# LSTM states stored batch-major, row loads spread over the first stage, and two norm steps moved, in a four-layer graph network

## The chip, the cores and the metric

The kernel runs on one core of one Trainium2 chip. The metric is the device time of one execution in microseconds (us). The kernel before takes 2278.68 us in the median of three runs (2278.61 to 2280.02).

The engines named below: TensorE (PE; PEld is its weight load), VectorE (DVE), ScalarE (ACT), GpSimd (POOL), and SyncE (SP), which here only issues DMAs. Each takes its instructions in the order in which the program holds them. SP and POOL have a DMA queue each.

## The reference, cut to what matters

The input `x` has 128 batches of 64 nodes with 256 features, float32 throughout; `adj` is 64 x 64. Four layers follow each other, and each adds its result to `x` and normalizes the rows.

```
x = layernorm(x + L0(x))   # three times: adj*adj applied to x @ W, relu between   (256 -> 512 -> 1024 -> 256)
x = layernorm(x + L1(x))   # U, the eigenvectors of the normalized Laplacian: U @ (relu(U.T @ x @ W1 + b1) @ W2 + b2)
x = layernorm(x + L2(x))   # below
x = layernorm(x + L3(x))   # attention between the 64 nodes, masked by adj
```

Layer 2, which holds the states that the change is about:

```
h = relu(adj @ (x @ Wg0 + bg0))
h = relu(adj @ (h @ Wg1 + bg1))
for p in 1, 2, 3, 4:                       # T = 64 nodes
    nw = T // p
    wins = h[:, :nw * p].reshape(B * nw, p, H)      # windows of p neighbouring nodes
    last = lstm_last(Wih[p], Whh[p], ..., wins)     # p steps, gates i, f, g, o; zero state first
    h[:, p - 1 : nw * p : p] = last                 # the last node of each window is replaced
```

So step t of a window of p nodes reads every p-th node of `h`, beginning with node t, and the last step's result is written to every p-th node.

## The kernel before, in words

**Rows and groups.** The 128 x 64 rows are 64 tiles of 128 rows (two batches each). Four tiles, eight batches, are a group; there are 16 groups. The rows of four groups stay in `X`, those of the other twelve are loaded to `XA` (lines 893 to 906).

**First stage: layer 0 and the eigenvectors.** `layer0` (line 1164) goes through the 16 groups in the order `order`, 4 to 15 and then 0 to 3. For each it computes the three products of layer 0, the two large ones by a scheme of seven block products in place of eight (`seven`, line 1101), which needs sums and differences of blocks. Those of the third product are made in the tile `sh`, of four slots, by DMA: SP copies one slot to another and a block of `h2` to a slot (lines 1182 and 1183), and POOL's queue issues DMAs that add to them (`adds`, line 1059). PE's product 5 of `by_third` (line 1097) is the first that reads `sh`. `mix_rows` (line 1138) adds the result to the rows, queues their normalization, and has SP store the rows of twelve groups to DRAM (`rest`, line 1153). In the gaps of PE and DVE runs `eigen` (line 275), a generator that computes the eigenvectors of the 64 x 64 matrix in small steps.

**Loads.** Before any of that the kernel issues all its loads on SP's queue (lines 910 to 959): the weights of layer 0, all 16 groups' rows in 128 KB pieces (`fetch`, line 904), then `eig_c` (constants of `eigen`), and the weights and biases of the later layers through `load` (line 888). The order of the instructions of PE, DVE, ACT and POOL in this stage is the order of the code (`tc.manual_schedule`, line 1227); SP's is chosen by the framework's scheduler.

**Second stage: layers 1 to 3.** The weights of the LSTMs are loaded, and then a planner (`Plan`, line 104) orders everything. Work is noted with a cost in us for each instruction (`Noted`, line 251; some have a `cost=` of their own), grouped in units of two groups of rows, and `Plan.run` (line 164) places up to four units' instructions by readiness and due time. Line 162, `emit`, therefore stands for all instructions of this stage in the profile. SP is planned too: loads and stores of rows, and `across` (line 1521), which sends a tile through DRAM to complete a transpose.

**The states.** `to_lstm` (line 1480) computes `h` transposed: features on the 128 partitions (two halves, `k`), and 512 columns for 64 nodes and 8 batches. These columns are stored node first: column 8n + b. The ReLU that writes them (`relu_out`, line 1500) turns them from batch-major, so it writes one element every 8. `singles`, `pairs` and `long` (lines 1774, 1781, 1791) run the LSTMs of windows of 1, 2, and 3 or 4 nodes; `long` takes the two groups of a unit at once. Each step is one call of `fast` (line 1679), which again uses seven products in place of eight on the two halves of features and two halves of columns: three of the seven read the state itself as the moving operand (the one that streams through PE, `moving[1..3]`), the others sums made by four subtractions on DVE. The hidden state `hs` between steps is a tile of its own and contiguous. The result goes to the state by `turn_out` (line 1770).

**Back to rows.** `from_lstm` (line 1534) turns the state to rows. For groups 0 to 13 DVE transposes 32 x 32 blocks, reading the state batch by batch (every 8th element), and `across` does the rest. For the last two groups, `ENDING`, the state is first copied batch-major, by two copies of DVE and two of ACT a group, and PE transposes the copy. `norm` (line 1434) normalizes two tiles: statistics on DVE, `(variance + eps) ** -0.5` on POOL in two steps (`rs`), and, for the last groups' `scalar` form, two more POOL steps for `nm`, minus the mean times `rs`, before ACT applies both.

Of the kernel before, what the change touches and what calls it, by code (L numbers as in the profile page):

```python
# [11 lines left out]
F32 = mybir.dt.float32  # L12
AF = mybir.ActivationFunctionType
ALU = mybir.AluOpType
# [762 lines left out]

RING = 4
QUADS = 1.17

# [60 lines left out]
def kernel(  # L841
# [74 lines left out]
    for h in range(2):  # L916
        cols = slice(h * 512, (h + 1) * 512)
        nc.sync.dma_start(aw2[:, :, cols], a_w2.rearrange("(k p) f -> p k f", p=P)[:, :, cols])
    for g in order[1:]:
        for u in range(2):  # L920
            fetch(nc.sync, g, u)
        if g == order[1]:
            aw3 = load(wa, "aw3", a_w3, "(k p) f -> p k f", [P, 8, D], p=P)
    nc.sync.dma_start(eig_c, consts)

# [24 lines left out]
    cb1 = keep.tile([P, 2], F32, name="cb1")  # L950
    nc.sync.dma_start(cb1, c_b1)
    wide = {}
    for name, src in (("b_b1", b_b1), ("b_b2", b_b2), ("c_b0", c_b0), ("d_b", d_b)):
        wide[name] = keep.tile([P, src.shape[0]], F32, name=f"wide_{name}")
        nc.sync.dma_start(wide[name], src.partition_broadcast(P))
    cbi = keep.tile([P, 4, 8], F32, name="cbi")
    cbh = keep.tile([P, 4, 8], F32, name="cbh")
    nc.sync.dma_start(cbi, c_bi)
    nc.sync.dma_start(cbh, c_bh)

# [203 lines left out]
    def layer0():  # L1164
# [12 lines left out]
        for g in range(n):  # L1177
            last = g == n - 1
            then = {} if last else {
                (1, 1): lambda: less(2, 0, 0),  # L1180
# [46 lines left out]
    with tc.manual_schedule(engines={mybir.EngineType.PE, mybir.EngineType.DVE, mybir.EngineType.Activation,  # L1227
                                     mybir.EngineType.Pool}):
        pt = bank()
        PE.transpose(pt[:N, :P], adst, ident)  # L1230
        for h in range(2):
            hs = slice(h * N, (h + 1) * N)
            V.tensor_copy(adT2[hs, hs], pt[:N, hs])
        V.tensor_mul(sqT2, adT2, adT2)
        layer0()
        while eig:
            now[0] = max(now[0], eig[0])
            between()
# [22 lines left out]
    few = ctx.enter_context(tc.tile_pool(name="few", bufs=1, reuse_waits="tile"))  # L1261
    psb = ctx.enter_context(tc.tile_pool(name="psb", bufs=1, space=bass.MemoryType.PSUM, reuse_waits="tile"))
    wih, whh = [], []
    for i in range(4):
# [169 lines left out]
    def norm(x, scalar, eps=EPS, twice=False):  # L1434
        st, mv, rs = plan.tile("st", [P, 2, 6]), plan.tile("mv", [P, 2, 2]), plan.tile("rs", [P, 2])
        for t in range(2):
            V.bn_stats(st[:, t, :], x[:, t, :])
            V.bn_aggr(mv[:, t, :], st[:, t, :])
        if twice:
            G.tensor_scalar(rs, mv[:, :, 1], eps, 0.25, op0=ALU.add, op1=ALU.mult)  # L1440
        else:
            G.tensor_scalar(rs, mv[:, :, 1], eps, None, op0=ALU.add)
        G.tensor_tensor(rs, rs, half[:, :2], ALU.pow, cost=0.74)
        if scalar:
            nm = plan.tile("nm", [P, 2])
            G.tensor_scalar(nm, mv[:, :, 0], -1.0, None, op0=ALU.mult)
            G.tensor_tensor(nm, nm, rs, ALU.mult)
        for t in range(2):
            if scalar:
                S.activation(x[:, t, :], x[:, t, :], AF.Identity, bias=nm[:, t:t + 1], scale=rs[:, t:t + 1], cost=0.5)  # L1450
            else:
                V.tensor_scalar(x[:, t, :], x[:, t, :], mv[:, t, 0:1], rs[:, t:t + 1], op0=ALU.subtract,
                                op1=ALU.mult)
# [26 lines left out]
    def to_lstm(xs, there):  # L1480
# [9 lines left out]
        a = mixed(g1, adT2)  # L1490
        hT = plan.tile("w", [P, 1024]).rearrange("p (k n b) -> p k n b", k=2, b=8)
        b = [[a[:, k, w * D:(w + 1) * D] for w in range(2)] for k in range(2)]
# [7 lines left out]
        def relu_out(c):  # L1500
            S.activation(hT[:, c, :, :].rearrange("p n b -> p b n"), hs[c].rearrange("p w (a n) -> p (w a) n", n=N),
                         AF.Relu, scale=2.0, cost=0.933)

# [30 lines left out]
    def from_lstm(xs, hT, g):  # L1534
        if g in ENDING:
            hb = as3(work(), 2)
            for bs in (slice(0, 4), slice(4, 8)):
                for k, copy, cost in ((0, V.tensor_copy, 0.33), (1, S.copy, 0.56)):
                    copy(as3(hb[:, k, :], 8)[:, bs, :], hT[:, k, :, bs].rearrange("p n b -> p b n"), cost=cost)
            for t in range(0, 4, 2):  # L1540
                p = ps4((P, 2, D))
                turns([(p[:, j, k * P:(k + 1) * P], hb[:, k, (t + j) * P:(t + j + 1) * P]) for j in range(2)
                       for k in range(2)])
                V.tensor_add(xs[:, t:t + 2, :], p, xs[:, t:t + 2, :])
                norm(xs[:, t:t + 2, :], True, 4 * EPS)
            return
        z = work()
        for k in range(2):
            V.transpose(z.rearrange("p (j t k f) -> p t j k f", j=4, t=4, k=2)[:, :, :, k],
                        hT[:, k].rearrange("p n b -> p b n"), cost=1.0)  # L1550
        y = across(z).rearrange("p (i m f) -> p m i f", i=4, m=8)
        for t in range(0, 4, 2):
            x2 = xs[:, t:t + 2, :].rearrange("p t (k i f) -> p (t k) i f", k=2, i=4)
            V.tensor_add(x2, y[:, 2 * t:2 * t + 4], x2)
            norm(xs[:, t:t + 2, :], False, 4 * EPS)
# [123 lines left out]
    def fast(p, n, x, hs=None, c=None, new=None, write=None):  # L1679
# [8 lines left out]
        def parts(v):  # L1688
            return v.rearrange("p (r b) -> p r b", b=8)

# [79 lines left out]
    def turn_out(dst, o, t):  # L1770
        o, t = (v.rearrange("p (r b) -> p r b", b=8) for v in (o, t))
        V.scalar_tensor_tensor(dst, o, 1.0, t, op0=ALU.add, op1=ALU.mult)

    def singles(hT):

        def write(h, o, t):
            turn_out(hT[:, h], o.rearrange("p w n -> p (w n)"), t.rearrange("p w n -> p (w n)"))

        fast(1, 256, [[hT[:, k, 32 * w:32 * w + 32, :] for w in range(2)] for k in range(2)], write=write)

    def pairs(hT):

        def write(h, o, t):
            turn_out(hT[:, h, 1:64:2, :], o.rearrange("p w n -> p (w n)"), t.rearrange("p w n -> p (w n)"))

        x = [[[hT[:, k, 32 * w + t:32 * w + 31 + t:2, :] for w in range(2)] for k in range(2)] for t in range(2)]
        c, hs = state("c"), state("hs")
        fast(2, 128, x[0], c=c, new=hs)
        fast(2, 128, x[1], hs=hs, c=c, write=write)

    def long(hTs, p):
# [3 lines left out]
        def seen(h, w, t):  # L1795
            return hTs[w][:, h, t:t + (nw - 1) * p + 1:p, :]

        def write(h, o, t):
            for w in range(2):
                turn_out(seen(h, w, p - 1), o[:, w], t[:, w])  # L1800

# [103 lines left out]
```

## Time and profile before

| what | value |
|---|---|
| median of three runs | 2278.68 us |
| profiled execution | 2278.08 us |
| its span, first to last instruction | 2276.3 us |
| mean granted TensorE clock | 0.991 |
| busy PE, PEld, DVE, ACT, POOL | 2215.7, 2035.9, 1758.0, 1241.8, 209.9 us |
| DMA | 163.10 MB, mean 72 GB/s |
| first stage | from 0 to some 822 us |
| second stage | from some 829 us to the end |

The span is what the profiled execution's engines did; 1.8 us of its time lie around it. PE's busy time counts each record of a matmul; a float32 matmul of this kernel is two records, each with a weight load of its own. Records overlap, so the spacing of their starts tells what one costs, and their duration is longer.

In the first two of the page's 40 slices (57 us each) 216 and 104 GB/s are moved, afterwards mostly 100 or less.

### The profile page before, as it was taken

To read this page: it belongs to the slowest core of one execution; us is meant where nothing else is said; L and a number is where in the kernel's file an instruction comes from. 1 tells how busy PE (TensorE), PEld (TensorE's weight loads), DVE (VectorE), ACT (ScalarE), POOL (GpSimd) and SP (SyncE) were. 2 spreads that over 40 slices of the span, in tenths; PEclk is the share of its full clock that TensorE was granted. 3 is DMA by queue.
4 is the path that set the end of the run, shared out by engine and by line. 5 is a ranking of instruction groups with operands and counts; after the bars stand their busy time and mean duration, and the time that the engine had idled before them with its cause. 6 is when DMAs were issued, how large, how long until landed. Compare 5 with 4: busy or idle time off the path is not lost.

```text
span 2276.3 us, 53986 instructions
## 1 busy us (share of the span) xinstructions
PE 2215.7 (97%) x21256; PEld 2035.9 (89%) x21256; DVE 1758.0 (77%) x5911; ACT 1241.8 (55%) x2999; POOL 209.9 (9%) x390
## 2 busy tenths in 40 slices
PE   8699999999999999999999999999999999999996
PEld 6688998888898878999999999999999999999995
DVE  6588878777888859765967977976976886668986
ACT  3255555545555445665655665655655656566554
POOL 0011111111111110000100000000010010000112
PEclk9899999999999999999999999999999999999998
DMA  7434333334433231000111211311221221002441
GB/s 216 104 93 100 87 76 85 78 81 101 96 85 75 66 135 48 20 1 20 66 44 37 85 57 42 94 57 41 87 66 41 78 75 38 13 11 71 130 122 44
DMA packets 95741, 163.10 MB, mean 72 GB/s; under 512 B 25472, under 2 KB 66432, under 8 KB 95488
## 3 DMA queue, kind: packets, MB, share of 16 engines
q1 hardware_dynamic: 84320, 120.05, 16.5%
q0 software_dynamic: 10800, 39.33, 9.1%
q8 instruction: 167, 2.74, 0.5%
q14 instruction: 86, 0.70, 0.1%
q10 hardware_dynamic: 368, 0.28, 0.0%
HBM read 57.64 MB, written 45.09 MB: 45 GB/s over the span
## 4 chain that ended last, share of the span: by engine, by line
PE 84%; DVE 8%; SPq 2%; DMA 2%; ACT 1%; issue 1%; POOL 1%; DVEq 0%; ACTq 0%; POOLq 0%
PE ps L162 55%; PE ch L977 15%; PE b L977 7%; PE ps L977 4%; PE ps L1070 2%; SPq L906 2%; DVE X L162 1%; DVE w L162 1%; DVE gates L162 1%; DVE D L52 1%; PE pa L312 1%; POOL rs L162 1%; DVE st L162 1%; PE ps L1143 1%; DMA aw<-in_a_w_dram 1%
## 5 line engine op out<-in xcount | busy, mean ns | idle before, releaser
L162 PE MATMUL ps<-w,wih 128*128 128x128 f32 (+2 forms) x2944 | 574.4, 299 | 4.7 <-DVE gates L162 2.0
L162 PEld LDWEIGHTS ps<-w,wih 128*128 128x128 f32 x2944 | 453.0, 191 | 32.4 <-DVE gates L162 6.8
L162 PE MATMUL ps<-w,sums 128*128 128x128 f32 (+2 forms) x3104 | 474.6, 294 | 0.2 <-DVE w L162 0.2
L162 PEld LDWEIGHTS ps<-w,sums 128*128 128x128 f32 x3104 | 421.9, 192 | 13.7 <-ACT gates L162 1.9
L162 ACT ACTIVATE gates<-gates,cbi 128x256 f32<-128x256 f32 (+4 forms) x736 | 318.0, 482 | 179.0 <-DVE gates L162 177.0
L162 DVE TENSOR_TENSOR gates<-gates,ps 128x512 f32<-128x512 f32 (+4 forms) x408 | 236.2, 586 | 159.0 <-PE ps L162 138.4
L162 ACT COPY gates<-ps 128x512 f32<-128x512 f32 (+4 forms) x408 | 205.2, 508 | 264.0 <-PE ps L162 258.8
L986 ACT ACTIVATE h<-h 128x512 f32<-128x512 f32 x141 | 89.0, 632 | 275.6 <-DVE h L52 275.0
L162 PE MATMUL ps<-hs,whh 128*128 128x128 f32 (+1 forms) x896 | 181.4, 284 | 0.2 <-DVE hs L162 0.2
L162 PE MATMUL ps<-w,whh 128*128 128x128 f32 (+1 forms) x896 | 181.2, 284 | 0.0
L162 POOL TENSOR_SCALAR rs<-mv 128x2 f32<-128x2 f32 x96 | 30.8, 329 | 1319.4 <-DVE mv L162 1317.7
L162 ACT ACTIVATE gates<-ps,cbi 128x128 f32<-128x128 f32 (+2 forms) x368 | 120.9, 385 | 40.9 <-PE ps L162 39.8
L162 PEld LDWEIGHTS ps<-hs,whh 128*128 128x128 f32 x896 | 139.7, 191 | 0.5 <-DVE hs L162 0.5
L162 PEld LDWEIGHTS ps<-w,whh 128*128 128x128 f32 x896 | 139.7, 191 | 0.0
L977 PE MATMUL b<-ss,aw 128*128 128x256 f32 x512 | 122.5, 379 | 0.0
L977 PE MATMUL ch<-m,tw 128*128 128x256 f32 x512 | 120.3, 380 | 0.0
L977 PEld LDWEIGHTS ch<-m,tw 128*128 128x128 f32 x512 | 96.4, 190 | 13.3 <-DVE h L52 0.4
L977 PEld LDWEIGHTS b<-ss,aw 128*128 128x128 f32 x512 | 96.5, 190 | 12.8
L1060 POOL DMA_DIRECT2D sh<-h x60 | 53.3, 959 | 503.9 <-ACT h L986 214.3
L162 PE MATMUL ps<-hs,sums 128*128 128x128 f32 (+1 forms) x448 | 90.6, 284 | 0.0
L162 ACT ACTIVATE gates<-c 128x256 f32<-128x256 f32 (+1 forms) x176 | 76.1, 435 | 24.5 <-DVE c L162 22.4
L162 DVE TENSOR_TENSOR w<-w,w 128x128 f32<-128x128 f32 (+2 forms) x264 | 79.6, 316 | 8.3 <-PE ps L162 6.6
(385 smaller groups left out, 4266.2 us busy)
## 6 DMA issues: line engine op xcount, KB each, us to landing
sh<-h POOLq DMA_DIRECT2D x60, 512.0 KB, 5.7
far<-w SPq DMA_DIRECT2D x42, 512.0 KB, 2.9
w<-far SPq DMA_DIRECT2D x168, 128.0 KB, 3.1
X<-rest SPq DMA_DIRECT2D x24, 512.0 KB, 3.7
out_dram<-X SPq DMA_DIRECT2D x64, 128.0 KB, 2.4
sh<-sh SPq DMA_DIRECT2D x15, 512.0 KB, 2.9
sh<-h SPq DMA_DIRECT2D x15, 512.0 KB, 2.9
sh<-sh POOLq DMA_DIRECT2D x15, 512.0 KB, 4.6
```

The source lines that it names most:

```text
L52: return getattr(self.engine, name)(out, *args, **kw)
L162: getattr(e, name)(*[real(x) for x in args], **{k: real(v) for k, v in kw.items()})
L312: PE.matmul(out, lhsT, rhs, start=True, stop=True)
L906: queue.dma_start(rows_of(g)[hs, 2 * u:2 * u + 2, :], given[2 * g + u, h])
L977: PE.matmul(out, lhsT, rhs, start=start, stop=stop, **kw)
L986: S.activation(dst, src, AF.Relu)
L1060: nc.gpsimd.dma_start(out, src, accum_op=ALU.add)
L1070: PE.matmul(p[h][m, k, t, :], src[hs, t, f], sqT2[hs, hs], start=True, stop=True)
L1143: PE.matmul(p[h][js, u, :], sqT2[hs, hs], s3[hs, 2 * u + j, :], start=True, stop=True)
```

## The change

The states are stored batch first, column 64b + n. The ReLU's write, the transposes of groups 0 to 13, and the transposes of the last groups then read or write contiguous columns, and the four copies a group before the latter are gone. In exchange a step's columns of a window of p nodes lie p elements apart: reads by PE and DVE and the writes of the last step.

In `norm`'s scalar form, `variance + eps` and `nm` (now one instruction) are on DVE; the power stays on POOL.

In the first stage only the first four groups' rows are loaded ahead (`AHEAD`). The others are issued at the head of the steps, four groups ahead, and so are the loads of constants, two a step. SP's order is now that of the code there too.

```diff
+AHEAD = 4
@@ loads
-    for g in order[1:]:
+    for g in order[1:AHEAD]:
         for u in range(2):
             fetch(nc.sync, g, u)
         if g == order[1]:
             aw3 = load(wa, "aw3", a_w3, "(k p) f -> p k f", [P, 8, D], p=P)
-    nc.sync.dma_start(eig_c, consts)
+    later = [(eig_c, consts)]
+
+    def load(pool, name, src, pattern, shape, **kw):
+        t = pool.tile(shape, F32, name=name)
+        later.append((t, src.rearrange(pattern, **kw)))
+        return t
...
-    nc.sync.dma_start(cb1, c_b1)
+    later.append((cb1, c_b1))
...
@@ layer0
         for g in range(n):
             last = g == n - 1
+            if g + AHEAD < n:
+                for u in range(2):
+                    fetch(nc.sync, order[g + AHEAD], u)
+            for to, of in later[2 * g:2 * g + 2]:
+                nc.sync.dma_start(to, of)
...
     with tc.manual_schedule(engines={mybir.EngineType.PE, mybir.EngineType.DVE, mybir.EngineType.Activation,
-                                     mybir.EngineType.Pool}):
+                                     mybir.EngineType.Pool, mybir.EngineType.SP}):
@@ norm
-        if twice:
+        if scalar:
+            V.tensor_scalar(rs, mv[:, :, 1], eps, None, op0=ALU.add)
+        elif twice:
             G.tensor_scalar(rs, mv[:, :, 1], eps, 0.25, op0=ALU.add, op1=ALU.mult)
         else:
             G.tensor_scalar(rs, mv[:, :, 1], eps, None, op0=ALU.add)
         G.tensor_tensor(rs, rs, half[:, :2], ALU.pow, cost=0.74)
         if scalar:
             nm = plan.tile("nm", [P, 2])
-            G.tensor_scalar(nm, mv[:, :, 0], -1.0, None, op0=ALU.mult)
-            G.tensor_tensor(nm, nm, rs, ALU.mult)
+            V.scalar_tensor_tensor(nm, mv[:, :, 0], -1.0, rs, op0=ALU.mult, op1=ALU.mult)
@@ to_lstm
-        hT = plan.tile("w", [P, 1024]).rearrange("p (k n b) -> p k n b", k=2, b=8)
+        hT = plan.tile("w", [P, 1024]).rearrange("p (k b n) -> p k b n", k=2, b=8)
...
-            S.activation(hT[:, c, :, :].rearrange("p n b -> p b n"), hs[c].rearrange("p w (a n) -> p (w a) n", n=N),
-                         AF.Relu, scale=2.0, cost=0.933)
+            S.activation(hT[:, c].rearrange("p b n -> p (b n)"), hs[c].rearrange("p w n -> p (w n)"), AF.Relu, scale=2.0)
@@ from_lstm
-            hb = as3(work(), 2)
-            for bs in (slice(0, 4), slice(4, 8)):
-                for k, copy, cost in ((0, V.tensor_copy, 0.33), (1, S.copy, 0.56)):
-                    copy(as3(hb[:, k, :], 8)[:, bs, :], hT[:, k, :, bs].rearrange("p n b -> p b n"), cost=cost)
             for t in range(0, 4, 2):
                 p = ps4((P, 2, D))
-                turns([(p[:, j, k * P:(k + 1) * P], hb[:, k, (t + j) * P:(t + j + 1) * P]) for j in range(2)
-                       for k in range(2)])
+                turns([(p[:, j, k * P:(k + 1) * P], hT[:, k, 2 * (t + j):2 * (t + j) + 2, :].rearrange("p b n -> p (b n)"))
+                       for j in range(2) for k in range(2)])
...
             V.transpose(z.rearrange("p (j t k f) -> p t j k f", j=4, t=4, k=2)[:, :, :, k],
-                        hT[:, k].rearrange("p n b -> p b n"), cost=1.0)
+                        hT[:, k].rearrange("p b n -> p (b n)"))
@@ pairs, long (singles alike, contiguous)
-            turn_out(hT[:, h, 1:64:2, :], o.rearrange("p w n -> p (w n)"), t.rearrange("p w n -> p (w n)"))
-        x = [[[hT[:, k, 32 * w + t:32 * w + 31 + t:2, :] for w in range(2)] for k in range(2)] for t in range(2)]
+            turn_out(hT[:, h, :, 1:64:2], *(v.rearrange("p w (b r) -> p (w b) r", b=4) for v in (o, t)))
+        x = [[[hT[:, k, 4 * w:4 * w + 4, t:63 + t:2] for w in range(2)] for k in range(2)] for t in range(2)]
...
-            return hTs[w][:, h, t:t + (nw - 1) * p + 1:p, :]
+            return hTs[w][:, h, :, t:t + (nw - 1) * p + 1:p]
```

## The prediction

> **What bounds the kernel now.** I read the page first: share of busy time by engine, then the 40 slices.
>
> ```profile
> PE 2215.7 (97%) x21256; PEld 2035.9 (89%) x21256; DVE 1758.0 (77%) x5911; ACT 1241.8 (55%) x2999; POOL 209.9 (9%) x390
> ...
> PE   8699999999999999999999999999999999999996
> ```
>
> TensorE is busy in 97% of the span, with holes only in the first two slices and in the last. So I asked for the busy time of seven stretches, cut where PE stops and resumes:
>
> ```profile
> 0.00:58.70 58.70, 50.38 (x444) 38.11 (x444) 38.24 (x157) 20.72 (x45) 1.02 (x9) 1.00 0.76 215
> 58.70:76.40 17.70, 0.01 (x1) 0.04 (x1) 1.72 (x11) 1.30 (x3) 3.70 (x4) 0.63 0.78 201
> 76.40:84.00 7.60, 7.60 (x43) 7.39 (x44) 4.00 (x19) 1.62 (x5) 0.86 (x1) 0.73 1.01 190
> 84.00:822.00 738.00, 734.42 (x6934) 654.55 (x6933) 600.57 (x2700) 375.02 (x915) 94.23 (x156) 1.00 0.35 82
> ...
> 830.00:2227.00 1397.00, 1385.95 (x13575) 1308.36 (x13565) 1081.11 (x2918) 816.51 (x1966) 96.58 (x181) 1.00 0.19 59
> 2227.00:2276.30 49.30, 30.32 (x200) 22.36 (x199) 30.85 (x105) 24.58 (x62) 12.05 (x36) 0.78 0.16 35
> ```
>
> After the stretch's length stand the busy times of PE, PEld, DVE, ACT and POOL, then the granted clock. Three things follow. PE stands still for 17.7 us from 58.7 on and then runs 7.6 us at clock 0.73. From 84 to 822 and from 830 to 2227 it is idle for 14.6 us in 2135, so nothing saved on DVE or ACT there shortens anything, while each nanosecond added to a PE record counts in full. The last 49 us are a chain in which PE is busy 61%.
>
> The hole, in order of time (start, length, engine, line, tile):
>
> ```profile
> 54.86 0.59 SPq L924 DMA_DIRECT2D eig_c<-in_consts_dram  x1
> ...
> 63.88 0.55 SPq L1182 DMA_DIRECT2D sh<-sh  x1
> 64.53 0.54 SPq L1183 DMA_DIRECT2D sh<-h  x1
> ...
> 68.83 2.06 POOL L1060 DMA_DIRECT2D sh<-h  x2 [67.23 <-DMA sh<-sh]
> ...
> 76.39 1.62 PE L977 MATMUL b<-tv,sh 128*128 128x128 f32 x6 [17.69 <-DMA sh<-h]
> ```
>
> SP issues all row loads and then the constants, one after the other, until 63.7 us. Only then come the two copies into `sh` of the first step; POOL's adding DMAs wait for them, and PE for those. Their inputs were there long before: ACT wrote the second half of `sh` slot 2 at 48.53 to 49.16.
>
> **The change, part by part.** All sums are against the profiled execution: 2278.08 us, span 2276.3. The median of the runs is 2278.68, 0.6 higher.
>
> *Loads spread.* SP now issues three groups ahead instead of fifteen, four row loads and two constants at each step. At the old pace (12 loads of the first three groups at 0.9 us each, 40 in 35.9 us, after 8.5 us) the queue reaches the first `sh` copy, with group four and two constants before it, by about 25 us, so the copy issues when ACT is done: 49.2, the second at 49.7. The price of the chain from there is in the second step, where no loads stand in front: second copy issued 115.64, POOL's add behind it 119.76, about 4 us. An add's landing took 5.9 us there. So the data of product 5 is there at 49.7 + 4 + 5.9 = 59.6, against 58.7 needed: 1 us of wait is left. With the old chain's whole length (63.88 to 76.39, 12.5 us) it would be 61.7, 3 us. I take 1, nearest to the row without loads. Gain 17.7 - 1 = 16.7. The slow stretch afterwards, 7.6 x (1 - 0.73) = 2.0, goes too, since the pause is short. **-18.7 us**; ends -20 (no wait left) and 0 (another wait holds PE to 76). What is late next: SP is now in written order, so each step's four loads and two constants (about 0.55 us an issue, 3.3 us) stand before the store of `rest` and the next `sh` copies. They are issued at the head of a step of some 49 us (738 us in 15 steps), wait for no engine and are needed two or more steps later; the step's first `sh` copy (107.35 in the second) waits for ACT anyway. POOL's queue is unchanged here.
>
> *Strided turns.* The 32 ReLU writes and 28 transposes become contiguous:
>
> ```profile
> L162 ACT ACTIVATE w<-v 128x512 f32<-128x512 f32 x32 | 36.0, 1136 | 13.2 <-DVE v L162 10.1 <-PE ps L162 2.9
> ...
> L986 ACT ACTIVATE h<-h 128x512 f32<-128x512 f32 x141 | 89.0, 632 | 275.6 <-DVE h L52 275.0
> ...
> L162 DVE STREAM_TRANSPOSE w<-w 128x512 f32<-128x512 f32 x28 | 29.9, 1096 | 0.0
> ...
> L162 DVE STREAM_TRANSPOSE w<-v 128x512 f32<-128x512 f32 x28 | 19.6, 702 | 13.7 <-PE ps L162 11.5 <-ACT v L162 2.1
> ```
>
> The second line is a contiguous ReLU of the same size. ACT saves 32 x 0.504 = 16.1 us, DVE 28 x 0.394 = 11.0 us. Both lie beside PE's 99.2%: **0**. If PE waited on each of them it would be at most the 11 us that PE idles in that stretch.
>
> *What takes their place.* This is the unknown. With batch outside, one time step of a window of 2, 3 or 4 nodes is read with every column 8, 12 or 16 bytes from the last; before, columns came in runs of eight. Three of the seven products (1, 2, 3) read the state itself, the others contiguous sums. By the code that is 21 matmuls of 128 columns a group for windows of two (3 products x 3+4 gates, 16 groups: 336), 33 of 168 a pair of groups for three (264), 45 of 128 for four (360); each float32 matmul is two records. Columns: 86,016 at 8 bytes, 88,704 at 12, 92,160 at 16. No PE row of this trace has such a read. From above: the DVE and ACT rows just shown pay 0.394/512 = 0.77 and 0.504/512 = 0.98 ns per element for jumps of 32 bytes, which would be 205 to 262 us over all, 71 to 90 for the 16-byte ones alone. From below 0; a gain is excluded, since contiguous records are the fastest rows there are. The nearest row on PE itself is today's read, which jumps already, once in eight columns:
>
> ```profile
> 1500.22 0.45 PE L162 MATMUL ps<-w,sums 128*128 128x168 f32 x2
> 1500.51 0.45 PE L162 MATMUL ps<-hs,sums 128*128 128x168 f32 x2
> 1500.79 0.45 PE L162 MATMUL ps<-w,sums 128*128 128x168 f32 x2
> 1501.08 0.45 PE L162 MATMUL ps<-hs,sums 128*128 128x168 f32 x2
> ```
>
> This is product 3 of a step of windows of three: `w` is the state, read with 21 jumps, `hs` is contiguous, and the starts are 0.28 or 0.29 us apart for two records behind either. PE's stream swallows those jumps. It takes a column in 0.143/168 = 0.85 ns, not faster than DVE or ACT, so it is no proof for a jump at each column. I take **0** because it is the only PE row, and keep 71, 90 and 262 for rivals and range. The Trainium skill speaks against the change here ("SBUF — State Buffer", section "Door 1: The DMA port swizzle"): accesses should hit a 16-byte line at least twice, and one to a new line each time pays. By that, steps of 8 bytes would be free, of 16 not; no row here shows a 16-byte step, and the sum by that rule would be the rival's below.
>
> On DVE the same reads stand in the four subtractions of a step (128 of 128, 96 of 168, 128 of 128 elements) and in 96 state writes (256, 168, 128): 66,560 elements, at most 0.77 ns each, 51 us, less the 11 saved. DVE would go from 1081 to 1121 of 1397 us; PE's backlog covers it: 0, at worst the few us by which a first product of a chain is later.
>
> *The end.* The eight batch copies of the last two groups go. In the chain that ended last they and their handover stand so:
>
> ```profile
> 2231.86 0.30 DVE w L162
> ...
> 2232.18 0.66 ACT w L162
> ...
> 2232.88 5.27 PE ps L162 x31
> ```
>
> The last state write ends at 2232.35, so the turns can start some 0.5 us earlier and no longer wait for ACT's four copies (until 2234.52): 0.5 to 1.3, I take **-0.9**. In eight norms three POOL steps beside the power (`rs`, two for `nm`; about 0.23 each, 0.07 between) become two on DVE. In the last norm (2269.44 to 2271.03) that saves about 0.5 us, as nothing is queued behind. In the others DVE stands for POOL's 0.71 us power, with the softmax steps behind it, and the new order puts the last two norms side by side, so that the last waits for two powers: +0.7. I take 0 for all norms, ends -1.5 (three on the chain, 0.5 each) and +2.1 (three blocked, 0.7 each).
>
> Sum: -18.7 - 0.9 = -19.6; 2278.08 - 19.6 = 2258.5 for such an execution, **2258** rounded.
>
> **The rivals.** (1) *A jump at each 16-byte step costs PE what it costs DVE and ACT.* For: three engines' worth of rows would then agree, and PE has no slack. Against: PE's stream shows nothing at runs of eight. 2258 + 71 to 90 = 2329 to 2348, slower. It decides from 19.6 us / 92,160 = 0.21 ns a column on. (2) *12-byte steps pay too*: + up to 68 to 87 more, 2397 to 2435; with 8-byte steps as well 2463 to 2520. (3) *The hole stays in part*: SP's written order, or the loads that now run beside the `sh` adds, keep half of the 18.7: 2268; the whole gone, 2277. For: SP waits up to 21.5 us for ACT's norms before a `rest` store. Against: that store stood before the same copies already.
>
> **How the numbers follow.** Chances: forecast (2249 to 2265, by the ends of the hole's wait and of the norms) 0.56; rival 3 0.07; a small PE price of 0.05 to 0.5 ns at 16-byte steps (2263 to 2304) 0.07, split between the signs; rival 1 0.17; rival 2 0.13. A measurement tells 0.2%, 4.6 us, from no change: faster 0.56 + 0.06 + 0.02 = 0.64, same 0.02, slower 0.34. The range leaves out 2 in 10: 2249 to 2348 leaves rival 2 and the forecast's and rival 1's edges.
>
> **What would show it.** Right: no PE hole after 58.7 longer than 3 us, the first `sh<-sh` issued near 49; transposes near 700 ns and the ReLU near 630; two `w,sums` records beside `hs,sums` still 0.28 us apart for 168 columns (0.22 for 128). Wrong: those spacings differ by the window's step, with PE's busy time up by tens of us between 830 and 2227.

## The result and the profile after

The changed kernel takes 2397.49 us in the median of four runs (2395.77 to 2400.93), the kernel before 2278.8 in four on the same chip. The ratio is 1.0525, with a 95% interval of 1.0512 to 1.0538: 119 us slower. The forecast was 2258, its range ended at 2348. The profiled span is 2395.9 us, 119.6 longer.

From the page of the changed kernel, the busy times and the slices of PE:

```profile
PE 2341.8 (98%) x21256; PEld 2134.5 (89%) x21256; DVE 1770.2 (74%) x5923; ACT 1232.4 (51%) x2995; POOL 203.5 (8%) x366
...
PE   8999999999999989999999999999999999999996
```

PE executes exactly as many records as before, 21256, but is busy 126.1 us longer, and its hole in the second slice is closed. So PE did not wait more; its records became longer. The busy time by stretches, changed kernel (PE, PEld, DVE, ACT, POOL, then the granted clock):

```profile
0.00:58.00 58.00, 49.90 (x443) 37.95 (x444) 37.80 (x155) 20.41 (x44) 4.71 (x13) 1.00 0.61 163
58.00:76.00 18.00, 17.23 (x295) 15.61 (x294) 14.47 (x72) 7.75 (x18) 0.86 (x1) 1.00 0.51 108
84.00:822.00 738.00, 724.71 (x6652) 643.64 (x6651) 585.80 (x2631) 366.68 (x897) 95.22 (x159) 0.99 0.38 91
830.00:2347.00 1517.00, 1505.19 (x13475) 1401.45 (x13466) 1092.62 (x2916) 808.80 (x1965) 95.14 (x181) 1.00 0.17 54
2347.00:2396.00 49.00, 29.68 (x223) 23.50 (x221) 31.53 (x118) 22.71 (x58) 7.09 (x12) 0.85 0.16 35
```

Three readings. Between 58 and 76 us, where PE had stood still, it is now busy for 17.2 of 18 us at full clock. Between 84 and 822 it is busy for 9.7 us less than before and has executed 282 records fewer. And the stretch from 830 to the final chain is 120 us longer (1517 against 1397) for nearly the same number of records. A boundary that holds for all kernels below is the first record of the second stage on PE (`ps<-u,X`): it starts at 828.58 us before and at 827.47 after. So the first stage gained 1.1 us in place of 18.7, and the second, to the end of the span, grew from 1447.7 to 1568.4 us, by 120.7.

**The second stage: the spacing of PE's records.** Timeline of PE in the kernel before, at a step of windows of four (start, duration):

```profile
1580.62 0.39 PE L162 MATMUL ps<-hs,whh 128*128 128x128 f32 x2
1580.85 0.39 PE L162 MATMUL ps<-w,wih 128*128 128x128 f32 x2
1581.07 0.39 PE L162 MATMUL ps<-hs,whh 128*128 128x128 f32 x2
```

The same kind of place in the changed kernel:

```profile
1564.10 0.62 PE L162 MATMUL ps<-w,wih 128*128 128x128 f32 x2
1564.53 0.40 PE L162 MATMUL ps<-hs,whh 128*128 128x128 f32 x2
1564.77 0.62 PE L162 MATMUL ps<-w,wih 128*128 128x128 f32 x2
...
1518.39 0.46 PE L162 MATMUL ps<-hs,whh 128*128 128x168 f32 x2
1518.68 0.61 PE L162 MATMUL ps<-w,wih 128*128 128x168 f32 x2
1519.13 0.46 PE L162 MATMUL ps<-hs,whh 128*128 128x168 f32 x2
```

A line with `w` beside `hs` is a read of the state itself (the other products with `w` read sums, which are contiguous). Before, two such records take 0.22 us to the next start, as all others of 128 columns do. After, they take 0.43 us where the window has four nodes, and 0.45 where it has three (168 columns; 0.285 before). The records beside them keep 0.24 and 0.29. Medians of the spacing per record between 1500 and 1700 us:

| columns, step | before | after | records | added |
|---|---|---|---|---|
| 128, 8 bytes | 0.110 us | 0.115 us | 672 | 3.4 us |
| 168, 12 bytes | 0.1425 us | 0.220 us | 528 | 40.9 us |
| 128, 16 bytes | 0.110 us | 0.215 us | 720 | 75.6 us |

The sum is 119.9 us, against 120.7 measured.

**The first stage: what took the hole's place.** The timeline of the changed kernel shows the first two copies of `sh` (`sh<-sh`, then `sh<-h`) and the adds in time, and product 5 without a wait for them:

```profile
37.45 0.54 SPq L1193 DMA_DIRECT2D sh<-sh  x1
...
47.62 0.51 SPq L1194 DMA_DIRECT2D sh<-h  x1
...
55.08 1.75 POOL L1066 DMA_DIRECT2D sh<-h  x2 [3.05 <-DMA sh<-h]
...
58.93 0.91 PE L983 MATMUL b<-tv,sh 128*128 128x128 f32 x6 [0.36 <-DVE q L52]
```

But its waits between 76 and 830 us hold three new ones on DVE (total, times, longest), and one on PE that follows from them:

```profile
DVE wide_c_b L1256 <- DMA wide_c_b<-in_c_b_dram: 4.2, 1, 4.2
DVE cbi L1257 <- DMA cbh<-in_c_bh_dram: 4.2, 1, 4.2
DVE dbb L1258 <- DMA dbb<-in_d_b_dram: 3.8, 1, 3.8
...
PE ps L983 <- DVE XA L52: 9.9, 3, 3.5
```

These are three small steps on the biases of later layers. The code writes them behind the first stage and outside the part whose order is fixed, so their place in DVE's order is the framework scheduler's; the changed kernel runs them at 159, some 264 and some 369 us, in the middle of the stage. Each waits there for a constant which SP issued at the head of a step (152.17, 258.25 and 362.32 us in the chain) and which takes 6 to 7 us to land. Behind the waiting step DVE's order holds `XA`, the result of a step, and behind that stands PE. The kernel before had the same three waits, between 60 and 70 us:

```profile
DVE dbb L1247 <- DMA dbb<-in_d_b_dram: 3.8, 1, 3.8
DVE wide_c_b L1245 <- DMA wide_c_b<-in_c_b_dram: 2.8, 1, 2.8
DVE cbi L1246 <- DMA cbh<-in_c_bh_dram: 0.5, 1, 0.5
```

They lay inside the hole, where PE stood anyway, and cost nothing. What a PE pause costs besides itself, in the stretches of the changed kernel around the first of the three:

```profile
157.00:160.00 3.00, 0.00 (x0) 0.00 (x0) 0.96 (x4) 0.00 (x0) 0.00 (x0) 0.83 1.06 201
160.00:164.00 4.00, 3.88 (x9) 3.17 (x10) 3.51 (x17) 2.47 (x9) 0.00 (x0) 0.50 0.61 122
164.00:168.00 4.00, 4.00 (x24) 3.62 (x24) 1.90 (x11) 2.00 (x6) 2.01 (x4) 0.78 0.00 0
...
126.00:176.00 50.00, 46.72 (x319) 41.00 (x318) 36.26 (x180) 22.85 (x61) 6.63 (x11) 0.93 0.41 96
```

Taken in stretches of 1 us, the clock is 0.50 from 159 to 165 us, 0.61 in the next and full from 166. After the second pause (3.5 us) PE works at half clock for some 5.8 us as well, after the third (3.2 us) for some 3. The Trainium skill ("TensorE: Matmul & The Clock Gate", section "What's actually happening") gives half the clock after an idle window of about 3.4 us; here a pause that the waits put at 3.2 us was enough.

**What the change did save.** Transposes and the ReLU on the changed kernel, groups by form:

```profile
L162 DVE STREAM_TRANSPOSE w<-w 128x512 f32<-128x512 f32 x28 | 18.8, 692 | 0.0
...
L162 ACT ACTIVATE w<-v 128x512 f32<-128x512 f32 x32 | 19.9, 623 | 23.1 <-DVE v L162 23.1
```

In all 11.1 and 16.1 us less than before, as forecast, and all of it beside a full PE.

### The profile page after: what moved, and what is told of

The parts are those of the page before. It is cut to its first block, busy times and chain, and to the rows that moved or that the text cites. A ratio compares the mean times of both kernels' runs of the same rounds, so it can differ in the third digit from the quotient of the medians.

```text
span 2395.9 us, 54054 instructions
## 1 busy us (share of the span) xinstructions
PE 2341.8 (98%) x21256; PEld 2134.5 (89%) x21256; DVE 1770.2 (74%) x5923; ACT 1232.4 (51%) x2995; POOL 203.5 (8%) x366
## 4 chain that ended last, share of the span: by engine, by line
PE 86%; DVE 8%; DMA 3%; ACT 1%; issue 1%; SPq 1%; POOL 0%; ACTq 0%; DVEq 0%
PE ps L162 58%; PE ch L983 14%; PE b L983 7%; PE ps L983 4%; PE ps L1076 2%; DVE w L162 1%; DVE v L162 1%; DVE D L52 1%; DVE X L162 1%; PE pa L312 1%; DMA w<-far 1%; DMA sh<-h 1%; DVE gates L162 1%; DVE tw L52 1%; PE ps L1149 1%
## 5 line engine op out<-in xcount | busy, mean ns | idle before, releaser
L162 PE MATMUL ps<-w,wih 128*128 128x128 f32 (+2 forms) x2944 | 658.4, 329 | 0.8 <-ACT w L162 0.6
L162 PE MATMUL ps<-w,sums 128*128 128x128 f32 (+2 forms) x3104 | 522.1, 308 | 0.4 <-DVE w L162 0.4
L162 PEld LDWEIGHTS ps<-w,wih 128*128 128x128 f32 x2944 | 464.9, 191 | 26.8 <-issue 1.9
L162 PEld LDWEIGHTS ps<-hs,whh 128*128 128x128 f32 x896 | 169.2, 199 | 14.9 <-DVE hs L162 0.6
L162 POOL TENSOR_SCALAR rs<-mv 128x2 f32<-128x2 f32 x88 | 22.2, 265 | 1405.6 <-DVE mv L162 1404.6
L1066 POOL DMA_DIRECT2D sh<-h x60 | 53.3, 958 | 494.3 <-ACT h L992 189.7
L162 DVE TENSOR_TENSOR w<-w,w 128x128 f32<-128x128 f32 (+2 forms) x264 | 90.3, 360 | 3.9 <-DMA far<-w 1.5
```

The costliest lines, as they stand in the source:

```text
L162: getattr(e, name)(*[real(x) for x in args], **{k: real(v) for k, v in kw.items()})
L1066: nc.gpsimd.dma_start(out, src, accum_op=ALU.add)
```

## The experiments

Twelve kernels. The second stage's length (first `ps<-u,X` to the end of the profiled span) is given for each, since the first stage varies by a few microseconds between executions:

| kernel | time, us | stage 2 starts | stage 2 lasts |
|---|---|---|---|
| before | 2278.8 | 828.6 | 1447.7 |
| after | 2397.5 | 827.5 | 1568.4 |
| old_layout | 2275.0 | 830.7 | 1443.5 |
| consts_early | 2258.7 | 812.3 | 1444.2 |
| layout_only | 2402.3 | 829.6 | 1571.0 |
| pe_runs | 2278.4 | 829.6 | 1447.0 |
| p4_step32 | 2403.8 | 830.5 | 1571.6 |
| p4_pairs0 | 2316.0 | 825.6 | 1488.6 |
| p4_pairs1 | 2323.5 | 833.3 | 1488.4 |
| p4_pairs3 | 2404.7 | 832.7 | 1570.2 |
| five_early | 2260.5 | 818.4 | 1443.7 |
| after_early | 2381.4 | 812.4 | 1567.2 |
| by_two | 2266.0 | 816.1 | 1453.8 |
| norm_only | 2276.7 | 828.7 | 1445.5 |

old_layout, consts_early, five_early, by_two and norm_only are medians of four to ten executions; the others below "after" are single ones.

### The parts apart

**old_layout**: the changed kernel with the node-first states put back (the ReLU, the copies at the end, the transposes and the reads and writes of the LSTMs as before).

```diff
-        hT = plan.tile("w", [P, 1024]).rearrange("p (k b n) -> p k b n", k=2, b=8)
+        hT = plan.tile("w", [P, 1024]).rearrange("p (k n b) -> p k n b", k=2, b=8)
...
```

> The changed kernel with the states stored node first again: the loads spread and the norm steps moved, the layout not. Theory A (the whole loss is PE's strided reading): the second stage falls back to some 1447 us from PE's first record of it to the end, and the time to 2276 to 2278, since the first stage of the changed kernel ended only 1.1 us earlier than before. Rival (the loads or the written order of SP also harm the second stage): above 2285.

Measured: 2274.96 us, ratio to the kernel before 0.9985 (0.9976 to 0.9995). DVE's three waits for constants are there as in the changed kernel (3.9, 4.2 and 4.3 us). So the loads as written, with the norms, bring next to nothing, and the whole loss belongs to the layout.

**layout_only**: the kernel before with the new layout, in all that reads and writes the state, and nothing else of the change.

```diff
-        hT = plan.tile("w", [P, 1024]).rearrange("p (k n b) -> p k n b", k=2, b=8)
+        hT = plan.tile("w", [P, 1024]).rearrange("p (k b n) -> p k b n", k=2, b=8)
...
```

> The kernel before with the layout changed alone. Theory A: PE pays about 0.105 us more a record at 16-byte steps (720 records), 0.078 at 12 bytes (528 of 168 columns), 0.005 at 8 bytes (672), 120 us together, so 2278 + 120 = 2398, less about 1 at the end. Rival (part of the loss comes from the loads or norms): clearly below 2390.

Measured: 2402.3 us, the second stage 1571.0, 123.3 longer than before: the layout alone makes the loss.

**consts_early**: old_layout, with the fifteen constants issued ahead of the first stage again; the rows stay spread.

```diff
     later.append((cbh, c_bh))
+    while later:
+        nc.sync.dma_start(*later.pop(0))
```

> As old_layout, but the fifteen loads of constants are issued ahead of the first stage's loop again, right after the first four groups' rows; only the rows stay spread. Theory B (in the changed kernel three small DVE steps, which wait for constants that now arrive late, stop DVE for 4 us each, PE behind it for 3.3 us each, and lower the clock after each): the three waits go, the first stage ends some 18 us earlier than before, total 2258 to 2261. Rival (the row loads that now run beside the adding DMAs cost the 17.6 us that the removed hole should have given): 2275 to 2278, as old_layout.

Measured: 2258.71 us (2257.84 to 2259.57), ratio 0.9912 (0.9897 to 0.9927). The three DVE steps now stand between 28 and 35 us, where they wait 4.4 us in all; from 76 to 830 us DVE waits for no constant, and the second stage starts 16.3 us earlier than before. The stretches of this kernel that answer to those with the pauses:

```profile
126.00:176.00 50.00, 49.89 (x478) 44.73 (x477) 41.84 (x209) 26.69 (x70) 6.69 (x11) 1.00 0.41 96
226.00:276.00 50.00, 50.00 (x497) 45.07 (x499) 42.54 (x214) 26.57 (x70) 6.67 (x11) 1.00 0.41 96
```

PE is full at clock 1.00 where the changed kernel had 46.7 us at 0.93. This version beats both kernels, the one before by 0.9%, clear of the noise.

**five_early**: as consts_early, but only the constants that the three DVE steps read (cbh, cbi, the wide c_b0, dbb, dbl) are issued ahead.

```diff
     later.append((cbh, c_bh))
+    for i in (14, 13, 11, 7, 6):
+        nc.sync.dma_start(*later.pop(i))
```

> The changed kernel with the node-first layout put back, and five of the fifteen late constants (dbl, dbb, the wide c_b0, cbi, cbh) issued ahead of the first stage, the other ten left spread. Theory: of the late constants only these have an early reader, the three DVE steps that the framework's scheduler puts into the middle of the first stage (dbb + dbl, wide c_b0 times rs_col, cbi + cbh); so this takes what all fifteen early took, 2258.7 us (2257 to 2261), and DVE waits for none of them in the first stage. Rival: it is the mere number of loads ahead of the first stage, or another constant; then some of the 16.3 us stays lost and the time lies between 2262 and 2275 us.

Measured: 2260.47 us (2257.88 to 2263.96), ratio 0.9919 (0.9904 to 0.9933), within the interval of consts_early, and no wait of DVE for a constant between 76 and 830 us. Ten of the fifteen can be late at no measured cost; the five could not. The profiled execution, the longest of the four, lost some 6 us between 20 and 76 us, where PE was busy for 47.6 us against 53.3 in consts_early. Its chain of work goes there through one of the five early constants:

```profile
27.07 4.48 DMA dbl<-in_d_bl_dram
...
31.64 0.16 DVE dbb L1260
...
33.85 2.67 PE ps L985 x8
```

Ahead of this stands a weight load (`aw`) that landed at 23.5 us, against 18.8 in consts_early, and SP issued the constants behind it. The three steps wait there 8.5 us for constants, against 4.4 in consts_early, so even early constants are on the path of this stretch; how much of the 6 us is theirs was not measured apart.

**after_early**: the changed kernel whole, with the fifteen constants early (the same two lines).

> The changed kernel whole, batch-first layout, with its fifteen constants issued ahead of the first stage. If the layout's loss lies only behind the first stage and the late constants' only in it, the two add: 2397.5 - 16.3 = 2381.2 us (2377 to 2386; chips differ by some us here). If the two hide each other, as where the start of the second stage is set by something else, it stays at 2390 to 2398 us.

Measured: 2381.37 us, 16.1 below the changed kernel, in a single execution. The two effects add.

**norm_only**: the kernel before with the norms' part alone.

```diff
+        if scalar:
+            V.tensor_scalar(rs, mv[:, :, 1], eps, None, op0=ALU.add)
...
-            G.tensor_scalar(nm, mv[:, :, 0], -1.0, None, op0=ALU.mult)
-            G.tensor_tensor(nm, nm, rs, ALU.mult)
+            V.scalar_tensor_tensor(nm, mv[:, :, 0], -1.0, rs, op0=ALU.mult, op1=ALU.mult)
```

> The kernel before with the norms' part of the change alone: the first step of the last norms on DVE, and the two steps for the negated mean on GpSimd made one on DVE. The prediction took 0 for it, between -1.5 and +2.1 us: 2277.2 to 2280.8 us against 2278.7. A rival from the node-first run, which came out 3.4 us ahead of the kernel before with the loads' part still mostly given back: the norms win those 3 us, 2275.5 us.

Measured: 2276.74 us, ratio 0.9991 (0.9982 to 1.0000): a gain between 0 and 4 us. The second stage is 2.2 us shorter than before, and in the two other pairs that differ by the norms in that stage (layout_only and after; before and old_layout) 2.6 and 4.2 us. By the times alone the sign is not beyond doubt. The chains that ended last help: they share a step of DVE on `gates`, here in the kernel before and then in the changed one:

```profile
2225.99 0.70 DVE gates L162
...
2348.74 0.70 DVE gates L162
```

From the start of this step to the end of the span it is 50.3 us before, 48.9 in norm_only, 50.0 in layout_only (the old norms) and 47.2 in the changed kernel. So the norms shorten this last stretch by 1.4 us alone and by 2.9 with the new layout, in single executions.

### Which engine pays for the layout

**pe_runs**: the changed kernel, but the three products that read the state stream contiguous runs of it, as many columns as before, though not the columns that the reference asks for; DVE's subtractions and writes stay strided.

```diff
-        moving = [None] + [[b[k][w] for b in ins] for k, w in ((0, 0), (1, 0), (1, 1))] + [T4, T1, T2, T3]
+        fed = [stream or x] + ins[1:]
+        moving = [None] + [[b[k][w] for b in fed] for k, w in ((0, 0), (1, 0), (1, 1))] + [T4, T1, T2, T3]
...
+            runs = [[hTs[w][:, k, :, nw * t:nw * t + nw] for w in range(2)] for k in range(2)]
+            fast(p, 8 * nw, x, hs, c, new, write, stream=runs)
```

> The changed kernel, but products 1 to 3 feed PE the same number of columns of the same state from contiguous runs (32, 21 and 16 columns), while DVE's subtractions and writes keep the strided columns. The products are therefore taken of other columns than the reference's. Theory A: PE's records cost 0.11 and 0.143 us again and the time falls by some 120 us to 2276 to 2279, DVE's strided reads notwithstanding. Rival (DVE's strided reads and writes, late for PE, carry a part): the time stays above 2290.

Measured: 2278.43 us. Groups of PE by form in this kernel (busy, mean ns of one):

```profile
L162 PE MATMUL ps<-w,wih 128*128 128x128 f32 x1856 | 328.9, 278 | 0.3 <-DVE gates L162 0.2
...
L162 PE MATMUL ps<-w,wih 128*128 128x168 f32 x704 | 148.2, 307 | 0.4 <-DVE gates L162 0.3
```

and in the changed kernel:

```profile
L162 PE MATMUL ps<-w,wih 128*128 128x128 f32 x1856 | 384.6, 310 | 0.0
...
L162 PE MATMUL ps<-w,wih 128*128 128x168 f32 x704 | 177.0, 350 | 0.1
```

(These groups hold other products as well; what a read of the state costs is in the table of spacings.) With PE's strided read 121.4 us of the second stage go. Against old_layout, which has the same norms, the changed kernel's is 124.9 us longer, so 3.5 us are left (1447.0 against 1443.5). So much at most is left for DVE's strided subtractions and writes, which are still there, give or take the 2 us by which single executions that ought to agree differ (1568.4 after, 1570.2 in p4_pairs3 below).

### What PE pays for

Of the changed kernel's reads only those for windows of four are changed here: 720 records, with as many columns, at other places. Three theories were to be told apart: a price for each line of 16 bytes that a record enters (LINES), one that grows with the step (DISTANCE), one for each long step (JUMPS).

**p4_step32**: columns 32 bytes apart in place of 16.

```diff
+        def look(h, w, t):
+            if p == 4:
+                return hTs[w].rearrange("p k b n -> p (k b n)")[:, 4 * h + t::8].rearrange("p (b r) -> p b r", b=8)
+            return seen(h, w, t)
...
-            x = [[seen(k, w, t) for w in range(2)] for k in range(2)]
+            x = [[look(k, w, t) for w in range(2)] for k in range(2)]
```

> The changed kernel, but in the windows of four PE reads x in columns 32 bytes apart where it had 16 (other columns than the reference's; as many of them, 720 records of 128 columns). Three theories of what PE pays for, all fitted to the spacing of records after the change (0.110 us for 128 columns 4 bytes apart, 0.115 for 8 bytes, 0.22 for 168 columns 12 bytes apart, 0.215 for 128 columns 16 bytes apart). LINES: a record takes the larger of 0.86 ns per column and 1.68 ns per 16-byte line that it enters; at 32 bytes every column enters one line, as at 16, so spacing 0.215 us and the time of the changed kernel, 2397 us. DISTANCE: the price per column goes on growing with the step (0.04, 0.46, 0.82 ns at 8, 12, 16 bytes), so at 32 bytes at least 1.6 ns, spacing 0.31 us and 2465 us. JUMPS: a fixed 0.82 ns for each step longer than 12 bytes: 0.215 us and 2397 us.

Measured: 2403.79 us, second stage 1571.6 against 1568.4; spacing 0.22 us per record where it was 0.215. A price that grows with the distance would have brought 2465 us: DISTANCE falls.

**p4_pairs0**, **p4_pairs1**, **p4_pairs3**: pairs of neighbouring columns, the next pair 32 bytes on; the pair begins at word 0, 1 or 3 of its eight (0:2 below, 1:3 and 3:5 in the other two). The rest of the edit is that of p4_step32.

```diff
+                return hTs[w][:, h].rearrange("p b n -> p (b n)").rearrange("p (c e) -> p c e", e=8)[:, :, 0:2]
```

> The changed kernel, but in the windows of four PE reads x as pairs of neighbouring columns, the next pair 32 bytes on, a pair in the first two words of its 32 bytes (other columns than the reference's; as many of them). LINES: half a line per column, 0.84 ns, below the 0.86 ns of a column: spacing 0.11 us, 720 x 0.105 = 75.6 us less than the changed kernel, 2322 us. JUMPS: 64 jumps of 0.82 ns in a record, 0.16 us, 37.8 us less, 2360 us. DISTANCE: the mean step is 16 bytes, as in the changed kernel, 2397 us, or, with the steps of 28 bytes priced like 32, half of them at 1.4 ns: 0.20 us, 2387 us.

> As the run with pairs in the first two words, but a pair lies in the second and third word of its 32 bytes (other columns than the reference's). LINES of 16 bytes: both words in one line, spacing 0.11 us, 2322 us. Were the lines 8 bytes long, each pair would enter two of them: 0.215 us and 2397 us. JUMPS: 0.16 us, 2360 us.

> As the runs with pairs, but a pair lies in the fourth and fifth word of its 32 bytes, so that it crosses from one 16-byte line into the next (other columns than the reference's). LINES of 16 bytes: every column enters a line of its own, spacing 0.215 us, 2397 us, 75 us above the other two pair runs though it reads as many columns at the same steps. Lines of 32 bytes: one line for a pair, 0.11 us, 2322 us. JUMPS: 0.16 us, 2360 us, as with the other pairs.

Measured: 2315.98, 2323.46 and 2404.69 us; second stages 1488.6, 1488.4 and 1570.2. Timelines of PE, first with the pair in words 1 and 2:

```profile
1545.75 0.40 PE L162 MATMUL ps<-w,wih 128*128 128x128 f32 x2
1545.98 0.38 PE L162 MATMUL ps<-hs,whh 128*128 128x128 f32 x2
1546.20 0.40 PE L162 MATMUL ps<-w,wih 128*128 128x128 f32 x2
```

then with the pair in words 3 and 4, across a border of 16 bytes:

```profile
1570.25 0.62 PE L162 MATMUL ps<-w,wih 128*128 128x128 f32 x2
1570.68 0.40 PE L162 MATMUL ps<-hs,whh 128*128 128x128 f32 x2
1570.92 0.62 PE L162 MATMUL ps<-w,wih 128*128 128x128 f32 x2
```

0.23 against 0.43 us for two records with the same steps, sizes and counts: only the place of the pair in its 16 bytes differs, and it decides 82 us. JUMPS, which expected 2360 us for all three, falls, and lines of 8 or 32 bytes with it. LINES stands: a record takes the larger of 0.86 ns per column (0.110/128) and 1.68 ns per line (0.215/128). At 8 bytes there are two columns in a line, 0.84 ns a column, hidden. At 12 bytes 21 columns enter 16 lines, eight times in a record: 128 lines, 0.215 us, where 0.22 was measured and contiguous reads take 0.1425.

**by_two**: a layout made from that. Early constants, and pairs of batches innermost, so that the state is read in runs of two words, never across a line; the turns on DVE and the ReLU on ACT go 8 bytes apart; the copies at the ends are back, and the last step for windows of three is written in four pieces.

```diff
-        hT = plan.tile("w", [P, 1024]).rearrange("p (k b n) -> p k b n", k=2, b=8)
+        hT = plan.tile("w", [P, 1024]).rearrange("p (k c n d) -> p k c n d", k=2, c=4, d=2)
...
-            return hTs[w][:, h, :, t:t + (nw - 1) * p + 1:p]
+            return hTs[w][:, h, :, t:t + (nw - 1) * p + 1:p, :]
...
```

> All fifteen constants early, and a third layout: k, then pairs of batches, node, the two batches of a pair innermost. PE then reads pairs of neighbouring words (8 bytes, never across a 16-byte line) with the next pair 16, 24 or 32 bytes on, the 28 turns and the ReLU of DVE and ACT read or write 8 bytes apart, and the copies at the ends are back. LINES (the larger of 0.86 ns per column and 1.68 ns per 16-byte line): half a line per column everywhere, records 0.11 to 0.115 us (128 columns) and 0.145 us (168), so no loss on PE; the turns fall from 1.1 to about 0.7 us and nothing of it reaches the end, since PE is full: 2258.7 us as with the constants early on the node-first layout, up to 0.005 us for each of 1920 records above it (2256 to 2268). JUMPS (0.82 ns for each step beyond the pair): 720 x 0.052 + 672 x 0.052 + 528 x 0.069 = 109 us more, 2367 us.

Measured: 2266.02 us (2263.18 to 2271.56), ratio 0.9938 (0.9921 to 0.9954). Groups by form in this kernel:

```profile
L162 DVE STREAM_TRANSPOSE w<-w 128x512 f32<-128x512 f32 x28 | 19.1, 698 | 0.0
...
L162 PE MATMUL ps<-w,wih 128*128 128x128 f32 x1856 | 333.1, 279 | 0.0
```

PE's loss is gone but for 0.115 and 0.15 us per record where runs of eight take 0.110 and 0.1425, and the turns are as fast as contiguous ones. The second stage is still 9.6 us longer than consts_early's: 1392 x 0.005 + 528 x 0.0075 = 10.9 us on a full PE. The 11 us saved on DVE bring nothing, so this layout gains nothing over node-first with early constants (ratios 0.9912 and 0.9919).

## Why the prediction was wrong

- **"What takes their place", taken at 0: this step failed.** It is 120 us. I had said what would decide, 0.21 ns a column at 16-byte steps, and measured are 0.82 (75.6 us for 92,160 columns), with 0.46 at 12 bytes (40.9) and 0.04 at 8 (3.4). The row that I took the 0 from, runs of eight columns with 21 jumps, was of the wrong kind: each run fills two whole lines, so it holds no column that enters a line alone and could not show the price. "The only PE row" was no reason to prefer it to the DVE and ACT rows, whose 71 to 90 us for the 16-byte steps hold the measured 75.6. The rule of two hits to a 16-byte line, which the prediction took from the Trainium skill ("SBUF — State Buffer", section "Door 1: The DMA port swizzle"), agrees with the pair runs, and I let one row outweigh it that did not test it. The same passage lets float32 stride for free up to 4 elements; the 16-byte steps measured here (0.215 us against 0.110) do not agree with that. The aside that PE takes a column "not faster than DVE or ACT" was misread too: its 0.85 ns stand against 1.37 (702 ns for 512) and 1.23 (632 ns).
- **"Loads spread", -18.7: the mechanism was right, the sum was not what the kernel got.** The hole went as worked out (second `sh` copy issued at 47.62 where 49.7 was expected, no wait for `sh` at product 5). The first copy went at 37.45, not near 49.2: the ACT step at 48.53, which I took for its input, writes another slot, and slot 2 was complete at 37.5. The sum did not suffer, since the second copy is the later one. What failed is the sentence that the loads and constants "wait for no engine and are needed two or more steps later". That holds for the rows and ten constants. Five are read by three DVE steps that the scheduler places a few microseconds behind their issue; I did not look where their readers stand. They took back 15.2 us (827.47 against 812.31): 9.9 are PE's waits, and the rest is put down to the halved clock behind each (some 14 us of work at 0.50 in the three; by an estimate from this, up to 7 us). With the constants early the gain was 16.3 us.
- **"Strided turns", 0: right.** Durations 692 and 623 ns against the 702 and 632 taken, and hidden.
- **DVE's strided reads, 0: right** within the 3.5 us that pe_runs leaves. DVE's busy time is 12 us above before's in the changed kernel, where up to 40 were allowed for.
- **The norms, 0 with ends -1.5 and +2.1:** measured -2.0, with an interval of -4 to 0. "The end", -0.9: with layout_only the last stretch, from the step on `gates`, is 0.3 us shorter (50.0 against 50.3), with the norms on top 3.1 (47.2).
- **The rivals.** Rival 2 named the mechanism, and its first figure, 2397, is the result; but it got there by two errors that cancel, 139 us at the least for the two steps (116.5 measured) and a gain of 19.6 at the loads and the end (1.1 measured in the first stage). Rival 3 had the gain lost by a hole that stays; the gain was lost, but the hole went, and DVE's waits for late constants took it back.

## What to carry to other kernels

When a layout is turned, look first at what the full engine reads: here each 16-byte line that PE's moving operand enters cost 1.68 ns, so two words from each line are nearly free (0.115 us a record against 0.110) and one from each doubles the record, while the savings on the engines beside it were worth nothing. A row proves that an access is free only if it has that access pattern; a run of eight is no test for a stride. When a load is moved later, look for the first reader of each tile in the order that the scheduler gives, not in the code: a bias read early on an in-order engine stops all that stands behind it.

## What the runs showed of the hardware

- Float32 moving operand of PE, 128 columns per record: 0.110 us contiguous or in runs of eight, 0.115 with two columns per 16-byte line, 0.215 to 0.22 with one, whether the step is 16 or 32 bytes. Only the border counts: a pair inside a line 0.115, the same pair across it 0.215.
- Three pauses of PE (3.2, 3.5 and 3.2 us) were each followed by work at granted clock 0.50, for some 5.7, 5.8 and 3.0 us; with 9.9 us of waits they went together with 15 us more in the first stage.
- DVE and ACT pay little at 8-byte steps: a 128x512 transpose reading 8 bytes apart took 698 ns, contiguous 692, 32 bytes apart 1096; ACT's ReLU writing so 674, 623 and 1136.
